# Score tiles of 32 queries and all four heads, PV packed to match, and a new hand-written order at both ends

## The chip, the cores and the metric

The kernel runs on one core of one Trainium2 chip. The metric is the time of one execution on the device in microseconds (us). Engines are named as the profile names them: PE (TensorE, matrix products), DVE (VectorE), ACT (ScalarE), POOL (GpSimd) and SP (SyncE, which here only issues transfers). The product of a 128x128 block of weights with N columns is "a matmul of N columns".

## The reference

Input `x` is (2, 512, 512): two batches, 512 tokens, 512 features. One layer follows: attention, residual and layernorm, then a feed-forward part, residual and layernorm.

```
q, k, v = x@Wq, x@Wk, x@Wv          # 32 query heads, 8 key/value heads of 128; 4 query heads share one k, v
scores  = q k^T * 128**-0.5,  causal mask,  probs = softmax(scores)
x = layernorm(x + (probs v) @ Wo)
w = sparsemax(x @ W_router^T + b_router)                       # 8 experts
x = layernorm(x + x@W_base^T + b_base + sum_e w_e (x A_e) B_e) # LoRA of rank 16 per expert
```

## The kernel before

**Precision.** Inputs and outputs are float32, and the kernel keeps nearly their precision with 16-bit products. Every operand is cut into a high part in fp16 and a low part (the rest, in fp16 too), scaled by powers of two that are found from maxima of the data. A product is then three matmuls into one PSUM tile: high x high, high x low, low x high (`mm3`, L229-232). Cutting a PSUM tile takes two instructions: ScalarE copies it to fp16 (L236), VectorE subtracts that from the original (L237).

**Groups and units.** A group is one key/value head of one batch, with its four query heads: 16 groups (g, b). A group has four units i = 0..3, one for each block of 128 queries; under the causal mask unit i needs the keys of blocks 0 to i. A unit goes through three stages:

- `unit_a` (L332): the scores, k against q. A score tile has 128 rows, which are **64 queries of two heads** (`R = P // 2`), so a unit has four tiles: heads 0 and 1 with the first 64 queries and with the last 64, then heads 2 and 3 likewise. The first sort is 128i+64 keys wide, the second 128i+128. For each tile: three matmuls into a PSUM tile of tag `S` (four buffers, so a unit fills them all); VectorE adds the mask and takes the row's extreme (L376); ScalarE takes the exponential and the row's sum (L381). After each pair of tiles `cut_p` follows: VectorE's reciprocals (L348, L350), ScalarE's high part of the normalized probabilities (L357), VectorE's low parts (L361, L363), all into the SBUF tile `phl`; then SP issues a DMA transpose of that half of `phl` to `pt` (L103). `phl` and `pt` have two buffers each, so every second unit uses the same one.
- `unit_b` (L396): PV, probabilities times v, in one PSUM tile (tag `PV`, one buffer). For the key blocks before the last, 3i matmuls of 512 columns. In the last block the first 64 queries need only 64 keys, so high and low part lie in one block of 128 rows: two matmuls of 256 columns, with copies of v packed accordingly (`vd`, `vz`); the last 64 queries take three of 256. The result is cut to `o2`.
- `unit_c` (L428): `o2` times Wo, twelve matmuls of 512 columns (`pw`), added to the accumulator `acc` by VectorE (L441).

**Between the stages.** While a group's units run, the next group's projections are computed from x: k and q of head 0 in unit 0, q1 in unit 1, v in unit 2, q2 and q3 in unit 3 (`proj`, L320). `turn_v` (L309) makes the packed copies of v on ScalarE in `v2` (4 parts of 512 columns) and transposes all 16 blocks of it in one DMA to `vt`. The cut q lies in tiles of two heads each (tag `Q`, three buffers). `factors` (L258) computes the groups' small scale factors `lm` on GpSimd.

**What sets the order.** The main loop (L899-925) calls, for unit s: `unit_a(s)`, the projections of the next group, `unit_b(s-1)`, `unit_c(s-2)`. A list `plan` (L821-851) says at which unit later weights are loaded (SP), measured (VectorE, L126, `mx`), and split (GpSimd, L120-123), and when the parts of the feed-forward block of batch 0 run (`ffn`, L643, a generator that goes on at each `step_live`). Within that, a scheduler decides each engine's order; loads on SP are held behind the third-last transpose (`hist[-3]`, L99). Each engine works through its own queue in order. Two stretches are ordered by hand instead (`tc.manual_schedule`): the **head** (L726-815), which loads x and the first weights and computes the first group's projections in float32 form before their scales are known (`park`), then their squares, maxima and scales; and the **tail** (L869), in which the last group's attention, the second batch's feed-forward block and the last block of the first batch are interleaved by the tokens of a string `TAIL` (L863). A token is a letter and a token block t: `a` scores, `p` their probabilities, `b`/`B` PV and `o`/`O` its cut, `q` a further half of the probabilities, `c`/`C` the product with Wo and `d`/`D` its sum, `n`/`N` statistics and normalizing, `x`/`X` and `l` the turn of the activations, `m` the base product (`pa`), `r` LoRA in (`pb`), `s` routing, `h` LoRA's middle (`phw`), `e` LoRA out, `f`/`F` last statistics and the store.

Of the kernel before, what the change touches and what calls it, by code (L numbers as in the profile page):

```python
# [8 lines left out]
F32 = mybir.dt.float32  # L9
F32R = mybir.dt.float32r  # L10
F16 = mybir.dt.float16
# [4 lines left out]
AX = mybir.AxisListType  # L16

P = 128
R = P // 2
NB, S, HID = 2, 512, 512  # L20
NT = S // P
KC = HID // P
NG = 8
HPG = 4
NE, NR = 8, 16
NL = NE * NR + NE
NQ = 3
SCALE = float(P) ** -0.5
NEG = -1.0e30
BIG = 3.0e38  # L30
# [11 lines left out]
def kernel(  # L42
# [33 lines left out]
    make_identity(nc, ident)  # L76
    mask = const.tile([P, S], F32, tag="mask", name="mask")
    nc.gpsimd.memset(mask, 0.0)
    for half in range(2):
        tri = mask[half * R : (half + 1) * R, S - R : S]  # L80
        nc.gpsimd.affine_select(
            out=tri, in_=tri, pattern=[[-1, R]], compare_op=ALU.is_ge, fill=NEG, base=0, channel_multiplier=1,
        )
    cmh = const.tile([P, 1], F32, tag="cmh", name="cmh")
    nc.gpsimd.memset(cmh, -0.5)
    v2 = const.tile([P, 4, S], F16, tag="v2", name="v2")
    nc.gpsimd.memset(v2[:, 3, :], 0.0)
    ones = const.tile([P, P], F32, tag="ones", name="ones")
    nc.gpsimd.memset(ones, 1.0)

# [11 lines left out]
    def sync_transpose(dst, src):  # L102
        hist.append(nc.sync.dma_start_transpose(dst, src).ins)  # L103
# [154 lines left out]
    def factors(g, b):  # L258

        lm = sb.tile([P, 8], F32, tag="lm", name=f"lm{g}_{b}", bufs=3)  # L260
        sc = SC[(g, False)]
        first = (g, b) == (0, 0)
        engine = nc.vector if first else nc.gpsimd
        engine.tensor_scalar(lm[:, 4:5], sc[:, 0, 4:5], XS[b][0], 1.0, ALU.mult, ALU.mult)  # L264

        step = 1 if first else 2
        for half in range(2):
            on = slice(half * R, (half + 1) * R)
            for p in range(0, 2, step):
                heads = slice(2 * p + half, 2 * p + half + 2 * step - 1, 2)  # L270
                engine.tensor_scalar(
                    lm[on, p : p + step], sc[on, 0, heads], lm[on, 4:5], -(2.0**-80), ALU.mult, ALU.min
                )
        LM[(g, b)] = lm

    def pj(name, tag="pj"):
# [16 lines left out]

    def end_q(g, b, h, pq):

        if h % 2 == 0:
            QT[(g, b, h // 2)] = sb.tile([P, 2, 2 * NT, 2, R], F16, tag="Q", name=f"q{g}_{b}_{h}", bufs=NQ)
        q2 = QT[(g, b, h // 2)][:, :, :, h % 2, :]
        return cut_psum(q2[:, 0], q2[:, 1], pq.rearrange("p (j q) -> p j q", q=R), cut(b, g, h))

    def mul_v(g, b, tag="pj"):
# [6 lines left out]

    def turn_v(g, b):  # L309

        first, twice = (v2[:, k : k + 2, :].rearrange("p a (t k) -> p a t k", k=P) for k in (0, 2))
        nc.scalar.copy(
            twice[:, 0].rearrange("p t (a k) -> p t a k", a=2), first[:, 0, :, :R].unsqueeze(2).broadcast_to([P, NT, 2, R])
        )
        nc.scalar.copy(twice[:, 1, :, :R], first[:, 1, :, :R])
        vt = sb.tile([P, 4 * NT, P], F16, tag="VT", name=f"vt{g}_{b}", bufs=2)
        sync_transpose(vt, v2.rearrange("p a s -> p (a s)"))
        VT[(g, b)] = vt

    def proj(g, b, j):  # L320
# [11 lines left out]
    def unit_a(g, b, i, whole=True):  # L332


        k2, lm = KT[(g, b)], LM[(g, b)]


        nb = 4 * i + 3
        phl = sb.tile([P, 2, nb * P], F16, tag="PHL", name=f"phl{g}_{b}_{i}", bufs=2)
        pt = sb.tile([P, 2, nb, P], F16, tag="PT", name=f"pt{g}_{b}_{i}", bufs=2)  # L340
        es = []
        st = sb.tile([P, 4, 4], F32, tag="ast", name=f"ast{g}_{b}_{i}", bufs=3)

        def keys(j):
            return i * P + (j + 1) * R

        def cut_p(h):
            nc.vector.reciprocal(st[:, 2, h : h + 2], st[:, 1, h : h + 2])  # L348

            nc.vector.scalar_tensor_tensor(  # L350
                st[:, 3, h : h + 2], st[:, 2, h : h + 2], 32768.0, es[h + 1][:, :2], ALU.mult, ALU.max
            )
            p = phl[:, h // 2]
            for j in range(2):
                n, src, by = keys(j), es[h + j], st[:, 3, h + j : h + j + 1]
                hi = p[:, j * (2 * i + 1) * P :][:, :n]
                nc.scalar.activation(hi, src[:, :n], AF.Copy, scale=by)  # L357
                lo = p[:, j * (2 * i + 1) * P + (i + 1) * P :][:, : i * P + j * P]
                m = lo.shape[1]
                if m:  # L360
                    nc.vector.scalar_tensor_tensor(lo, src[:, :m], by, hi[:, :m], ALU.mult, ALU.subtract)  # L361
                if m < n:
                    nc.vector.scalar_tensor_tensor(  # L363
                        p[:, n : n + R], src[:, m:n], by, hi[:, m:n], ALU.mult, ALU.subtract
                    )

            sync_transpose(pt[:, h // 2], p)

        for h in range(4):
            j = h % 2  # L370
            n, qs = keys(j), 2 * i + j
            q2 = QT[(g, b, h // 2)]
            qh, ql = (q2[:, a, qs].rearrange("p a q -> p (a q)") for a in range(2))
            sc = ps.tile([P, S], F32, tag="S", name=f"s{g}_{b}_{i}_{h}", bufs=4)
            mm3(sc[:, :n], [(qh, k2[:, 0, :n]), (qh, k2[:, 1, :n]), (ql, k2[:, 0, :n])])
            nc.vector.tensor_tensor_reduce(  # L376
                out=sc[:, :n], in0=sc[:, :n], in1=mask[:, S - n :], scale=lm[:, h // 2 : h // 2 + 1], scalar=BIG,
                op0=ALU.add, op1=ALU.min, accum_out=st[:, 0, h : h + 1],
            )

            nc.scalar.activation(  # L381
                sc[:, :n], sc[:, :n], AF.Exp, bias=st[:, 0, h : h + 1], scale=-1.0, accum_out=st[:, 1, h : h + 1]
            )
            es.append(sc)
            if whole and h % 2:
                cut_p(h - 1)
        PT[(g, b, i)] = pt
        yield
        if not whole:
            for h in (0, 2):  # L390
                cut_p(h)
                yield
# [3 lines left out]
    def unit_b(g, b, i):  # L396
        vt = VT[(g, b)]
        pt = PT.pop((g, b, i))
        pt = pt.rearrange("p e k (h q) -> p e k h q", q=R)
        pv = ps.tile([P, HPG, 2, R], F32, tag="PV", name=f"pv{g}_{b}_{i}")  # L400
        dst = pv.rearrange("p (e h) j q -> p j e h q", e=2)
        m = 2 * i + 1
        pairs = []
        for kt in range(i):
            ph, pl = (pt[:, :, k :: m][:, :, :2].rearrange("p e j h q -> p j e h q") for k in (kt, i + 1 + kt))
            vh, vl = vt[:, kt, :], vt[:, NT + kt, :]
            pairs += [(vh, ph), (vh, pl), (vl, ph)]
        if i:
            mm3(dst, pairs, last=False)

        vh, vl, vd, vz = (vt[:, k * NT + i, :] for k in range(4))
        both = pt[:, :, i]
        mm3(dst[:, 0], [(vd, both), (vz, both)], i == 0, i == 0)
        ph, pl = pt[:, :, m + i], pt[:, :, m + 2 * i + 1]
        mm3(dst[:, 1], [(vh, ph), (vh, pl), (vl, ph)], i == 0)
        yield
        o2 = sb.tile([P, 2, HPG, 2, R], F16, tag="O", name=f"o{g}_{b}_{i}", bufs=2)
        cut_psum(o2[:, 0], o2[:, 1], pv, 2.0**-15)
        OT[(g, b, i)] = o2
        yield  # L420
# [215 lines left out]
        mm3(PA[t], pairs, first=False)  # L636

    def store(t, src, st):
        y = sb.tile([P, HID], F32, tag="y", name=f"y{t}", bufs=2)
        normalize(y, src, st)  # L640
        nc.sync.dma_start(out_rows[t], y)

    def ffn(t):  # L643
# [9 lines left out]
        with behind(mybir.EngineType.PE):  # L653
            lora_in(t, False)
        route(t)
        yield
        yield
        lora_mid(t, False)
# [67 lines left out]
    with tc.manual_schedule(engines={ET.PE, ET.DVE, ET.Activation, ET.Pool, ET.SP}):  # L726
# [56 lines left out]
        end_q(0, 0, 0, PK[0])  # L783
        factors(0, 0)
        end_q(0, 0, 1, PK[1])
        for c in (2, 3):
            x_hi(1, c)
            x_lo(1, c, nc.gpsimd)
        park(2, "S")
        for c in range(KC):  # L790
            x_max(1, c)
        amax(mx[:, 7:8], mx[:, 13:17])
        end_v(0, 0, PK[5])
        park(3, "S")
        for k in range(4):
            w_squares(mx[:, 17 + k : 18 + k], wo_raw[k], "S")
        amax(sq1[:, 1:2], mx[:, 17:21])
        nc.scalar.activation(sq1[:, 0:1], mx[:, 7:8], AF.Square)
        end_q(0, 0, 2, PK[2])
        tot = total(sq1, 2, "1")  # L800
        convert = split_x(0, x0_raw)
        next(convert)
        turn_v(0, 0)
        end_q(0, 0, 3, PK[3])
        sc1 = sb.tile([P, 2, 8], F32, tag="sc1", name="sc1")
        scales(sc1, tot, 2)
        SC[(0, True)] = sc1[:, :, 1:3]
# [53 lines left out]


    TAIL = """  # L863
    n3 a7 N3 p7 B7 q7 O7 X3 l3 C6 D6 a6 r3 s3 p6 C7 q6 b7 D7 o7 h3 a5 m3 p5 q5 c7 d7 b6 n7 e3 o6
    a4 c6 N7 p4 q4 d6 X7 l7 n6 b5 m7 o5 f3 r7 c5 s7 N6 d5 h7 X6 n5 b4 e7 l6 o4 f7 F3 N5 r6 s6 F7
    c4 d4 X5 l5 n4 m6 h6 r5 m5 e6 s5 N4 f6 h5 X4 e5 l4 F6 r4 f5 s4 F5 m4 h4 e4 f4 F4
    """

    def tail():  # L869
# [112 lines left out]
```

## Time and profile before

| | |
|---|---|
| median of 3 runs | 677.68 us (677.02 to 681.1) |
| the profiled execution | 677.5 us, of which the span of its instructions is 675.4 us |
| granted TensorE clock | 0.999 of full speed |
| instructions PE / DVE / ACT / POOL | 3594 / 1698 / 1052 / 373 |
| busy DVE in 60-580 us and behind 580 us | 407.07 of 520 us, 77.68 of 96 us |
| busy PE in 60-580 us and behind 580 us | 518.36 of 520 us, 83.50 of 96 us |
| idle time of VectorE ended by a load of Wo, before a maximum (L126) | 21.6 us, 10 times |

Times are those of one execution that the hardware profiler recorded. A line that names a group of instructions gives the program's line, the engine, the operation, output <- input with shapes (partitions x elements) and the count. "Busy" of PE is not PE at its peak: the ends of matmuls are modelled and reach over the start of the next one. In lines of waits the three numbers are the idle time in all, how often, and the longest. In lines of a timeline the first two numbers are start and length in us; in square brackets stands the idle time before and what ended it.

### The profile page before, as it was taken

How to read it: one execution, taken by the hardware profiler on the slowest of the kernel's cores; microseconds unless marked ns; L12 is line 12 of the kernel's file. 1: busy time of each engine (PE TensorE's matmuls, PEld its weight loads, DVE VectorE, ACT ScalarE, POOL GpSimd, SP SyncE). 2: the span in 40 equal slices, each digit the busy share in tenths (PEclk: the TensorE clock that was granted, in tenths of full speed). 3: DMA queues.
4: the chain of work that ended last, by engine and by line, in shares of the span. 5: the costliest groups of instructions: out<-in, count | busy, mean ns of one | idle time of the engine just before them, and what ended most of it. 6: DMA issues, size and time to landing. Idle time of an engine off the chain costs nothing.

```text
span 675.4 us, 11524 instructions
## 1 busy us (share of the span) xinstructions
PE 656.8 (97%) x3594; PEld 348.6 (52%) x3594; DVE 531.6 (79%) x1698; ACT 369.5 (55%) x1052; POOL 250.3 (37%) x373
## 2 busy tenths in 40 slices
PE   8999999999999999999999999999999999999995
PEld 5755545455554545445554555555454545544452
DVE  6887788778696688678787797969777687878796
ACT  6876664746365764646464464726565465444520
POOL 4676450624117298623308067054405011100011
PEclk9999999999999999999999999999999999999999
DMA  8669393637539383635629454743726362453311
GB/s 313 203 153 164 96 192 74 147 62 131 134 68 215 92 207 59 137 70 110 156 41 207 109 104 103 151 116 73 156 44 123 40 130 47 92 117 74 71 44 47
DMA packets 205341, 78.89 MB, mean 117 GB/s; under 512 B 189920, under 2 KB 190176, under 8 KB 205280
## 3 DMA queue, kind: packets, MB, share of 16 engines
q1 hardware_dynamic: 205280, 78.17, 53.3%
q8 instruction: 28, 0.46, 0.3%
q14 instruction: 33, 0.27, 0.1%
HBM read 29.12 MB, written 2.10 MB: 46 GB/s over the span
## 4 chain that ended last, share of the span: by engine, by line
PE 74%; DVE 13%; DMA 4%; ACT 4%; issue 2%; POOL 2%; SPq 0%; POOLq 0%; ACTq 0%; DVEq 0%
PE pw L232 19%; PE pq L232 19%; PE pv L232 11%; PE s L232 11%; PE pk L232 5%; PE pvp L232 5%; PE pa L232 3%; DVE phl L361 2%; ACT s L381 2%; DVE s L376 1%; DMA raw<-in_wo_dram 1%; PE park L232 1%; DVE mx L126 1%; DVE acc L441 1%; DMA xraw<-in_xt_dram 1%
## 5 line engine op out<-in xcount | busy, mean ns | idle before, releaser
L381 ACT ACTIVATE s<-s,ast 128x192 f32<-128x192 f32 (+7 forms) x256 | 120.9, 472 | 149.8 <-DVE ast L376 143.9
L232 PE MATMUL pw<-w,o 128*128 128x512 f16 x768 | 176.9, 379 | 0.3 <-DVE o L237 0.3
L232 PEld LDWEIGHTS <-w 128*128 128x128 f16 x1008 | 98.1, 98 | 110.6
L232 PE MATMUL pq<-xT,w 128*128 128x512 f16 x672 | 152.1, 379 | 0.0
L357 ACT ACTIVATE phl<-s,ast 128x192 f16<-128x192 f32 (+7 forms) x256 | 110.7, 512 | 23.0 <-DVE ast L350 20.6
L361 DVE SCALAR_TENSOR_TENSOR phl<-s,ast,phl 128x128 f16<-128x128 f32 (+2 forms) x224 | 112.5, 515 | 8.0 <-ACT phl L357 7.4
L376 DVE CUSTOM_DVE_ANT_0 s<-s,mask,lm 128x192 f32<-128x192 f32 (+7 forms) x256 | 117.9, 519 | 0.0
L232 PEld LDWEIGHTS <-o 128*128 128x128 f16 x768 | 74.8, 98 | 77.2 <-DVE o L237 1.0
L232 PE MATMUL s<-k,q 128*128 128x320 f16 (+7 forms) x768 | 106.6, 286 | 3.3 <-DVE phl L363 1.9
L232 PE MATMUL pv<-pt,vt 128*128 128x256 f16 (+1 forms) x608 | 107.7, 323 | 1.5 <-DMA pt<-phl 1.0
L232 PEld LDWEIGHTS <-q 128*128 128x128 f16 x768 | 64.2, 98 | 45.1 <-DVE phl L363 3.3
L264 POOL TENSOR_SCALAR lm<-sc,xs 128x1 f32<-128x1 f32 x15 | 4.0, 267 | 220.6 <-DVE sc L140 111.5
L232 PEld LDWEIGHTS <-vt 128*128 128x128 f16 x608 | 59.2, 99 | 50.4 <-issue 2.0
L123 POOL TENSOR_TENSOR w<-raw,w 128x512 f16<-128x512 f32 x70 | 79.6, 1157 | 0.3
L441 DVE SCALAR_TENSOR_TENSOR acc<-pw,lm,acc 128x512 f32<-128x512 f32 x64 | 47.7, 745 | 22.8 <-PE pw L232 22.5
L120 POOL TENSOR_SCALAR raw<-raw,sc 128x512 f32<-128x512 f32 x70 | 47.9, 694 | 47.0 <-issue 36.2
L237 DVE SCALAR_TENSOR_TENSOR o<-pv,o 128x512 f16<-128x512 f32 x64 | 43.8, 684 | 24.8 <-ACT o L236 24.8
L126 DVE TENSOR_REDUCE mx<-raw 128x1 f32<-128x512 f32 x68 | 44.4, 677 | 21.6 <-DMA raw<-in_wo_dram 21.6
L236 ACT ACTIVATE o<-pv 128x512 f16<-128x512 f32 x64 | 39.5, 617 | 37.3 <-PE pv L232 37.1
L381 ACT ACTIVATION_READ_ACCUMULATOR s<-s,ast 128x1 f32 x256 | 51.3, 200 | 0.0
L237 DVE SCALAR_TENSOR_TENSOR q<-pq,q 128x512 f16<-128x512 f32 x56 | 37.9, 683 | 10.7 <-ACT q L236 10.4
L236 ACT ACTIVATE q<-pq 128x512 f16<-128x512 f32 x56 | 34.1, 614 | 21.2 <-PE pq L232 21.1
(170 smaller groups left out, 652.5 us busy)
## 6 DMA issues: line engine op xcount, KB each, us to landing
raw<-in_wo_dram SPq DMA_DIRECT2D x32, 256.0 KB, 3.9
raw<-in_wq_dram SPq DMA_DIRECT2D x29, 256.0 KB, 4.2
xraw<-in_xt_dram SPq DMA_DIRECT2D x8, 256.0 KB, 5.2
raw<-in_wk_dram SPq DMA_DIRECT2D x8, 256.0 KB, 3.5
raw_x<-in_xt_dram SPq DMA_DIRECT2D x8, 256.0 KB, 4.9
acc<-in_x_dram SPq DMA_DIRECT2D x8, 256.0 KB, 5.1
pt<-phl SPq DMA_TRANSPOSE x128, 3.6
out_dram<-y SPq DMA_DIRECT2D x8, 256.0 KB, 2.0
```

What stands on the lines that cost most here:

```text
L120: nc.gpsimd.tensor_scalar(view, view, by, 1.0, ALU.mult, ALU.mult)
L123: return first.ins, nc.gpsimd.tensor_tensor(lo, view, hi, ALU.subtract).ins
L126: nc.vector.tensor_reduce(dst, view, AX.X, ALU.max, apply_absolute_value=True)
L232: nc.tensor.matmul(dst, a, b, start=first and j == 0, stop=last and j == n - 1)
L236: nc.scalar.activation(hi, psrc, AF.Copy, scale=by)
L237: return nc.vector.scalar_tensor_tensor(lo, psrc, by, hi, ALU.mult, ALU.subtract).ins
L264: engine.tensor_scalar(lm[:, 4:5], sc[:, 0, 4:5], XS[b][0], 1.0, ALU.mult, ALU.mult)
L357: nc.scalar.activation(hi, src[:, :n], AF.Copy, scale=by)
L361: nc.vector.scalar_tensor_tensor(lo, src[:, :m], by, hi[:, :m], ALU.mult, ALU.subtract)
L376: nc.vector.tensor_tensor_reduce(out=sc[:, :n], in0=sc[:, :n], in1=mask[:, S - n :], scale=lm[:, h // 2 : h // 2 + 1], scalar=BIG, op0=ALU ...
L381: nc.scalar.activation(sc[:, :n], sc[:, :n], AF.Exp, bias=st[:, 0, h : h + 1], scale=-1.0, accum_out=st[:, 1, h : h + 1])
L441: nc.vector.scalar_tensor_tensor(a, pw, LM[(g, b)][:, 7:8], a, ALU.mult, ALU.add)
```

## The change

**Score tiles.** `R` is now 32. A score tile has the **32 queries of all four heads** in its 128 rows, and the four tiles of a unit are four successive blocks of 32 queries, 128i+32, +64, +96 and +128 keys wide. All heads' q go into one tile (tag `Q`, two buffers), and the four scale factors, which were two columns for two pairs of heads, are one column written in four quarters of the partitions: two operations more on GpSimd.

**Probabilities.** `phl` and `pt` become one tile each of 4m+2 blocks of 128 columns, with m = 2i+1. The first two tiles of a unit share the last key block: tile 0 has 32 keys there, written three times by ScalarE beside one low part; tile 1 has 64 keys high and 64 low. Tiles 2 and 3 have a whole block for high and for low each; the 32 columns that tile 2 does not fill in these two are zeroed by a ScalarE copy at the start of `unit_a`. A unit still has two transposes, of 2m and of 2m+2 blocks (before: 2m+1 each).

**V and PV.** `v2` has a fifth part, with v's first 32 keys of a block for the fourfold packing, and two more ScalarE copies fill it; its transpose has 20 blocks instead of 16. PV takes 3i matmuls of 256 columns for tiles 0 and 1, one of 128 columns for tile 0's last keys, two of 128 for tile 1's, and 3(i+1) of 256 for tiles 2 and 3.

**Orders.** In the head, `park(2)` and `park(3)` and the cuts of q2 and q3 stand elsewhere, and the squares of Wo are taken in two pairs. In the first group of each batch V's transpose is held behind the last transpose issued. `ffn` has one `yield` more before LoRA's middle. The stored result takes buffers of tag `rawo`. `TAIL` has a new order.

```diff
-R = P // 2
+R = P // 4
-    v2 = const.tile([P, 4, S], F16, tag="v2", name="v2")
+    v2 = const.tile([P, 5, S], F16, tag="v2", name="v2")
...
+        for h in range(HPG):
+            on = slice(h * R, (h + 1) * R)
+            engine.tensor_scalar(lm[on, 0:1], sc[on, 0, h : h + 1], lm[on, 4:5], -(2.0**-80), ALU.mult, ALU.min)
...
-        if h % 2 == 0:
-            QT[(g, b, h // 2)] = sb.tile([P, 2, 2 * NT, 2, R], F16, tag="Q", name=f"q{g}_{b}_{h}", bufs=NQ)
-        q2 = QT[(g, b, h // 2)][:, :, :, h % 2, :]
+        if h == 0:
+            QT[(g, b)] = sb.tile([P, 2, HPG * NT, HPG, R], F16, tag="Q", name=f"q{g}_{b}", bufs=2)
+        q2 = QT[(g, b)][:, :, :, h, :]
...
     def turn_v(g, b):
+        nc.scalar.copy(twice.rearrange("p t (a k) -> p t a k", a=2), double(2, r))
+        nc.scalar.copy(once[:, :, :r], low[:, :, :r])
+        nc.scalar.copy(four.rearrange("p t (a k) -> p t a k", a=4)[:, :, ::3], double(2, R))
+        nc.scalar.copy(four[:, :, R:r], low[:, :, :R])
+        vt = sb.tile([P, 5 * NT, P], F16, tag="VT", name=f"vt{g}_{b}", bufs=2)
+        with tc.issue_after(hist[-1]) if g == 0 and hist else nullcontext():
+            sync_transpose(vt, v2.rearrange("p a s -> p (a s)"))
...
     def unit_a(g, b, i, whole=True):
+        m = 2 * i + 1
+        nb = 4 * m + 2
+        phl = sb.tile([P, nb * P], F16, tag="PHL", name=f"phl{g}_{b}_{i}", bufs=2)
+        nc.scalar.copy(
+            phl.rearrange("p (k a) -> p k a", a=P)[:, 2 * m + i : 2 * m + m + 1 : i + 1, 3 * R :],
+            mask[:, : 2 * R].rearrange("p (k a) -> p k a", k=2),
+        )
...
+                if j > 1:
+                    high(p[:, :n], src[:, :n])
+                    low(lows[:, :n], 0, n)
+                    continue
+                if j:
+                    high(p[:, :n], src[:, :n])
+                else:
+                    if i:
+                        high(p[:, :full], src[:, :full])
+                    high(
+                        p[:, full : full + 3 * R].rearrange("p (a k) -> p a k", a=3),
+                        src[:, full:n].unsqueeze(1).broadcast_to([P, 3, R]),
+                    )
+                if i:
+                    low(lows[:, :full], 0, full)
+                low(p[:, full + (3 - j) * R : full + P][:, : n - full], full, n - full)
+            on = slice(0, 2 * m) if h == 0 else slice(2 * m, nb)
+            sync_transpose(pt[:, on], phl[:, on.start * P : on.stop * P])
...
+        for j in range(4):
+            n = full + (j + 1) * R
+            qh, ql = (q2[:, a, HPG * i + j].rearrange("p h q -> p (h q)") for a in range(2))
...
     def unit_b(g, b, i):
+        for kt in range(i):
+            pairs += three(kt, 0, m)
         if i:
-            mm3(dst, pairs, last=False)
+            mm3(dst[:, :2], pairs, last=False)
+        mm3(dst[:, 0], [(four, p0)], i == 0, i == 0)
+        mm3(dst[:, 1], [(twice, p1), (once, p1)], i == 0)
+        pairs = []
+        for kt in range(i + 1):
+            pairs += three(kt, 2 * m, m + 1)
+        mm3(dst[:, 2:], pairs)
...
-        y = sb.tile([P, HID], F32, tag="y", name=f"y{t}", bufs=2)
+        y = sb.tile([P, HID], F32, tag="rawo", name=f"y{t}", bufs=4)
...
         route(t)
         yield
         yield
+        yield
         lora_mid(t, False)
...
         end_q(0, 0, 1, PK[1])
+        park(2, "S")
         for c in (2, 3):
             x_hi(1, c)
             x_lo(1, c, nc.gpsimd)
-        park(2, "S")
+        park(3, "S")
+        for k in range(2):
+            w_squares(mx[:, 17 + k : 18 + k], wo_raw[k], "S")
         for c in range(KC):
             x_max(1, c)
         amax(mx[:, 7:8], mx[:, 13:17])
+        end_q(0, 0, 2, PK[2])
         end_v(0, 0, PK[5])
-        park(3, "S")
-        for k in range(4):
+        for k in (2, 3):
             w_squares(mx[:, 17 + k : 18 + k], wo_raw[k], "S")
         amax(sq1[:, 1:2], mx[:, 17:21])
         nc.scalar.activation(sq1[:, 0:1], mx[:, 7:8], AF.Square)
-        end_q(0, 0, 2, PK[2])
         tot = total(sq1, 2, "1")
+        end_q(0, 0, 3, PK[3])
...
-        end_q(0, 0, 3, PK[3])
...
     TAIL = """
-    n3 a7 N3 p7 B7 q7 O7 X3 l3 C6 D6 a6 r3 s3 p6 C7 q6 b7 D7 o7 h3 a5 m3 p5 q5 c7 d7 b6 n7 e3 o6
-    a4 c6 N7 p4 q4 d6 X7 l7 n6 b5 m7 o5 f3 r7 c5 s7 N6 d5 h7 X6 n5 b4 e7 l6 o4 f7 F3 N5 r6 s6 F7
-    c4 d4 X5 l5 n4 m6 h6 r5 m5 e6 s5 N4 f6 h5 X4 e5 l4 F6 r4 f5 s4 F5 m4 h4 e4 f4 F4
+    n3 a7 C6 N3 B7 p7 q7 O7 X3 l3 D6 a6 r3 C7 s3 b7 p6 q6 D7 h3 o7 m3 a5 p5 c7 b6 q5 e3 d7 o6 n7
+    a4 c6 N7 p4 q4 b5 f3 X7 l7 m7 o5 r7 d6 n6 s7 c5 N6 d5 h7 X6 n5 l6 b4 e7 o4 f7 r6 c4 N5 F7 s6
+    F3 X5 l5 d4 n4 m6 h6 r5 m5 s5 N4 e6 f6 h5 X4 l4 F6 e5 r4 s4 f5 m4 h4 F5 e4 f4 F4
     """
```

## The prediction

> **What bounds the kernel.** I read the page's first part, then the chain that ended last, then TensorE's instructions in order of time over one steady group, then what TensorE waited for.
>
> ```profile
> PE 656.8 (97%) x3594; PEld 348.6 (52%) x3594; DVE 531.6 (79%) x1698; ACT 369.5 (55%) x1052; POOL 250.3 (37%) x373
> PE 74%; DVE 13%; DMA 4%; ACT 4%; issue 2%; POOL 2%; SPq 0%; POOLq 0%; ACTq 0%; DVEq 0%
> ```
>
> TensorE is busy for 97% of the span and carries 74% of the chain; VectorE (79%) is next. The clock is granted in full. The group from 200.21 us, in order of time (start, length, engine, line, matmul, count):
>
> ```profile
> 200.21 2.59 PE L232 MATMUL s<-k,q 128*128 128x448 f16 x12
> 202.64 5.34 PE L232 MATMUL pq<-xT,w 128*128 128x512 f16 x24
> 207.82 2.00 PE L232 MATMUL pv<-pt,vt 128*128 128x512 f16 x11
> 209.66 2.75 PE L232 MATMUL pw<-w,o 128*128 128x512 f16 x12
> 212.25 0.67 PE L232 MATMUL s<-k,q 128*128 128x64 f16 x12
> 212.76 2.75 PE L232 MATMUL pk<-xT,w 128*128 128x512 f16 x12
> ...
> 217.94 2.65 PE L232 MATMUL pv<-pt,vt 128*128 128x512 f16 x14
> 220.43 2.75 PE L232 MATMUL pw<-w,o 128*128 128x512 f16 x12
> ...
> 226.76 0.71 PE L232 MATMUL pv<-pt,vt 128*128 128x256 f16 x5
> 227.31 2.75 PE L232 MATMUL pw<-w,o 128*128 128x512 f16 x12
> ```
>
> Lengths hold the pipeline's end, so I go from start to start: the scores of unit 3 (5,760 columns) take 202.64 - 200.21 = 2.43 us, those of unit 0 (1,152 columns) 0.51 us. That is 1.92 us for 4,608 columns, **0.417 ns a column**, and (510 - 480) / 12 = **2.5 ns a matmul**. Nothing else: no row waits for its weights. A 512-column matmul is then 216 ns, and twelve are the 2.59 us of pw. So in the middle of the run the time is a sum of columns. The waits that TensorE does have:
>
> ```profile
> PE s L232 <- DVE phl L363: 1.9, 4, 1.1
> PE phw L628 <- DVE hw L619: 1.6, 2, 1.4
> PE px L567 <- DVE phl L363: 1.3, 1, 1.3
> ...
> PE tot L131 <- ACT q L236: 1.1, 1, 1.1
> PE s L232 <- DVE q L237: 1.0, 1, 1.0
> PE pv L232 <- DMA pt<-phl: 1.0, 1, 1.0
> ```
>
> Nearly all lie in the first 60 us and behind 580 us; between, some 2 us, most at 289 us.
>
> **Scores.** Unit i had tiles of 128i+64 and 128i+128 columns, each twice, three matmuls to a tile: 13,824 columns in a group of four units. Now it has 128i+32, +64, +96, +128: 13,056. The count stays at 48. -768 x 0.417 = -0.32 us a group. The 32-column matmul has no row before: between 16 ns (by the two rates) and 29 ns (the 64-column one, 64 x 0.417 + 2.5). [...] **-0.29 us a group.**
>
> **PV.** Before, 3i matmuls of 512 and five of 256: 14,336 columns, 38 matmuls in a group. Now 3i of 256, one and two of 128 for the packed last keys, 3(i+1) of 256: 13,824 columns, 60 matmuls. -512 x 0.417 + 22 x 2.5 ns = -0.21 + 0.06 = **-0.16 us a group.** Sum -0.45, times 16 groups: **-7.2 us**, and the path runs through it.
>
> [...]
>
> **Other engines, steady part.** VectorE: mask and low parts lose 64 columns each a unit, about 0.13 us by its rows (619 to 754 ns for 384 to 512 columns, 1.05 ns a column): -0.5 us a group, same count. ScalarE gains a high part in three of four units (the 96-column copy, near the 371 ns row of 128 columns, about 0.27 us of its own time), a 128x64 copy of zeros in each unit (nearest row 317 ns at 64 columns) and two copies a group for V (409 and about 330 ns): 3 x 0.3 + 4 x 0.27 + 0.7 = 2.7 us, less 0.5 for narrower tiles. 55% becomes about 61%: costs nothing by itself. GpSimd gets two more small operations a group (295 ns), hidden at 37%.
>
> **New order of waits.** (a) Each score tile now needs all four heads, so the first needs what the third needed: 0.26 us earlier. The cover is PV and pw, 4.4 us; in most groups the last q is done 2.9 us ahead, but not in groups that prepare weights:
>
> ```profile
> 201.22 2.72 SPq L103 DMA_TRANSPOSE vt<-v  x1
> 207.08 0.69 DVE L126 TENSOR_REDUCE mx<-raw 128x1 f32<-128x512 f32 x1 [3.09 <-DMA raw<-in_wo_dram]
> 211.75 0.68 DVE L237 SCALAR_TENSOR_TENSOR q<-pq,q 128x512 f16<-128x512 f32 x1
> ```
>
> A maximum waits on VectorE for Wo's load, which stands on SP's queue behind V's transpose; the last q follows at 212.43, scores start at 212.25. V's transpose grows from 16 to 20 blocks: 2.72 / 4 = +0.7 us on SP, for the loads and the unit's own transposes behind it. Against it, in the built order of the changed program one of the two maxima between the low parts has gone behind the last q (0.6 us), and the low parts are 0.1 shorter. Net 0, and the 0.26 remains in six or so groups, 1.6 us, of which VectorE's lighter load of 0.5 us a group should take the larger part: between -1.5 (the stall at 289 goes) and +4, I take **+0.5 us**.
>
> (b) ScalarE's copy of zeros waits for the transposes of two units earlier, and stands ahead of exponentials. For unit 0 the exponentials began at 215.70 and the transpose in question landed at 217.26; over the groups that is 0 to 4.4 us, about 1.9. Behind it on ScalarE stand that unit's exponentials, high parts, k and q; for them wait VectorE's cuts, then the next unit's scores for PSUM. Those begin at 223.02, the cuts ended at 220.0: 3.0 us of cover here (3.3 to 5.8 elsewhere). I take 0; if cover were gone it is the first rival.
>
> **Beginning.** In the first group the scores also wait for head 3, whose cut now follows the second sum's squares; the sum's matmul waits about 1.2 us longer (VectorE finishes the maxima and two cuts first), and VectorE's v and q cuts stand ahead of it. Against that, all four tiles are ready together, the cut of the second half no longer waits behind a maximum for w1 (0.97 us), and the 1.0 us that PV waited for its transpose is mostly covered, since pvp is whole and one score ahead of it. **-0.5 us** (-1.5 to +1.5).
>
> **End.** By the new order the nine pvp matmuls (1.9 us) come ahead of phw (wait 1.4), PV ahead of pa (0.4), pw ahead of px (1.25; pw is 2.6), thirteen pa ahead of the scores that waited 1.1, and the last routing ahead of statistics (0.2). That is 4.4 us of TensorE waits. But from 603 us VectorE carries the chain, and pa moved behind seven PV matmuls is 1.0 us later in its line while VectorE waits 2.89 us for it at 605.94. So I count 1.4 + 0.4 - 1.0 = 0.8 for the first two, nothing for the next two, 0.5 for VectorE's smaller tiles in six units, and 0.2 for the routing: 0.8 + 0.5 + 0.2 = **-1.5 us** (0 to -4.4). The store's buffer change costs nothing: those raw buffers are long read.
>
> **Sum.** The profiled execution took 677.5 us, 675.4 of span and 2.1 around it; the median of the runs is 677.68, the same. 677.5 - 7.2 + 0.5 - 0.5 - 1.5 = **668.8 us**.
>
> **Rivals.**
> *Slower: ScalarE's queue becomes the bound.* The zeros' copy holds exponentials until a transpose lands that is itself 0.7 us later, on an engine with 2.2 us more work a group. It decides from where the delay, 1.9 us on average, passes the 3 us cover at unit 1's scores. In its favour: one group has 4.4 us. Against it: the groups with long delays have 5.8 us of cover. If 15 groups lost 1.2 us each, 668.8 + 18 = 686.8 us. It is slower as soon as the loss passes 0.6 us a group. 8%.
> [...] 6%.
> *The orders bring nothing* and (a) costs its upper end: 677.5 - 7.2 + 2 = 672.3 us, between 670.5 and 674. 23%.
> *The end gains all it can*, and the 289 us stall goes: 677.5 - 7.2 - 1 - 1 - 4 = 664.3 us. 15%.
> *The change doesn't do what it says*: the order shows the new widths and counts, so hardly.
>
> **Chances.** The forecast (666 to 670.5) has 48%. About 1% of the time is what a measurement can tell: below 670.9 is faster. 48 + 15 + 10 of the third rival's 23 give 0.73 faster, 13 + 6 give 0.19 within, 0.08 slower. The range that leaves out a fifth: 663.5 to 674.5.
>
> **What would show it.** A group's period falls from 38.0 to about 37.5 us. Start to start, scores take about 0.46 / 1.07 / 1.71 / 2.35 us by unit and PV 0.50 / 1.15 / 1.80 / 2.46. [...] If TensorE's waits name VectorE's low parts or q at each group's start, and ScalarE shows idle time ahead of the copy of zeros ended by a transpose, the first rival holds. TensorE's waits behind 580 us fall by 2 to 4 us if the new end works. I am wrong if some engine writes the 32-element runs of q, or TensorE PSUM's 32-column runs, slower than the 64-element ones of before; nothing in the trace speaks of it.

## The result and the profile after

The changed kernel is **slower**: 708.94 us (median of 6, 704.85 to 709.86) against 677.56 us before (6 runs), ratio 1.0444, 95% interval 1.0409 to 1.0478. The forecast was 668.8 us. The sign is that of the first rival (ScalarE's queue), which had been given 8% and 686.8 us.

The profiled execution took 709.86 us, 707.7 of span. Of its page, the busy times and the chain that ended last:

```profile
PE 664.8 (94%) x3946; PEld 376.0 (53%) x3946; DVE 521.2 (74%) x1698; ACT 386.9 (55%) x1196; POOL 258.5 (37%) x405
PE 16%; DVE 12%; ACT 7%; DMA 6%; issue 2%; POOL 1%; POOLq 0%; ACTq 0%; DVEq 0%; SPq 0%
```

TensorE's share falls from 97% to 94%. The chain, which could be followed over less than half of the span here, no longer runs along TensorE alone: DMA has 6%, and its costliest step is `pt<-phl`, the transpose of the probabilities. What TensorE waited for (idle time in us, times, longest):

```profile
PE s L231 <- DVE q L236: 12.9, 8, 2.6
PE s L231 <- ACT q L235: 5.2, 6, 1.9
PE s L231 <- DVE phl L368: 4.7, 11, 0.9
PE pq L231 <- DVE q L236: 2.9, 1, 2.9
```

Before, these sums were 1.0 us for q and 1.9 for phl. The scores wait for q, the projections too, since q's PSUM is not read in time. And what ScalarE waited for, the two longest entries:

```profile
ACT phl L347 <- DMA pt<-phl: 164.0, 52, 8.1
...
ACT s L400 <- DVE ast L395: 70.3, 36, 7.2
```

L347 is the new copy of zeros. Before, no transpose stood in the list, and its first entry was the exponentials' ordinary wait for VectorE:

```profile
ACT s L381 <- DVE ast L376: 143.9, 60, 4.7
```

Here is the group that the prediction showed, ScalarE in order of time (start, length, and in brackets the idle time before and what ended it):

```profile
205.88 0.24 ACT L347 CAST phl<-mask 128x64 f16<-128x64 f32 x1 [1.89 <-DMA pt<-phl]
206.03 0.47 ACT L400 ACTIVATE s<-s,ast 128x288 f32<-128x288 f32 x1
...
209.99 0.65 ACT L235 ACTIVATE v<-pvp 128x512 f16<-128x512 f32 x1
...
213.68 0.58 ACT L400 ACTIVATE s<-s,ast 128x416 f32<-128x416 f32 x1 [1.24 <-DVE ast L395]
...
215.69 0.24 ACT L347 CAST phl<-mask 128x64 f16<-128x64 f32 x1 [1.31 <-DMA pt<-phl]
215.84 0.60 ACT L400 ACTIVATE s<-s,ast 128x448 f32<-128x448 f32 x1
...
217.76 2.47 ACT L365 ACTIVATE phl<-s,ast 128x384 f16<-128x384 f32 x5
220.07 1.13 ACT L235 ACTIVATE q<-pq 128x512 f16<-128x512 f32 x2
```

The copy stands ahead of unit 2's exponentials (206.03) and again between the first two of unit 3 (215.84), each time ended by the landing of the transposes that read the same phl buffer. Both traces have a landmark in this group, the small `tot` sum on TensorE. Here it and the first exponential of unit 2, from the trace before, and the landmark in the changed kernel:

```profile
194.03 0.50 ACT L381 ACTIVATE s<-s,ast 128x320 f32<-128x320 f32 x1 [1.63 <-DVE ast L376]
196.29 0.28 PE L131 MATMUL tot<-sq,ones 128*128 128x6 f32 x2
```

```profile
205.22 0.28 PE L130 MATMUL tot<-sq,ones 128*128 128x6 f32 x2
```

Counted from the landmark, unit 2's exponentials start 3.1 us later than before (0.81 us behind it, where they were 2.26 us ahead), and everything behind them on ScalarE follows: v, its copies, V's transpose, q2 and q3. On TensorE:

```profile
218.96 2.75 PE L231 MATMUL pw<-w,o 128*128 128x512 f16 x12
221.55 0.20 PE L231 MATMUL s<-k,q 128*128 128x32 f16 x2
224.36 0.87 PE L231 MATMUL s<-k,q 128*128 128x32 f16 x10 [2.61 <-DVE q L236]
225.02 4.18 PE L231 MATMUL pk<-xT,w 128*128 128x512 f16 x12
229.04 2.75 PE L231 MATMUL pq<-xT,w 128*128 128x512 f16 x12
```

Two things are to be seen. The scores wait 2.61 us for q. And the twelve matmuls of pk that follow take 4.02 us from start to start where twelve are worth 2.59 us. The same stretches with the granted clock (third figure from the end; window, its length, then busy time of each engine):

```profile
221.50:224.40 2.90, 0.29 (x5) 0.14 (x4) 2.90 (x7) 0.19 (x1) 2.90 (x5) 1.00 0.47 91
225.00:229.10 4.10, 4.10 (x16) 1.63 (x14) 3.28 (x13) 0.24 (x1) 1.21 (x2) 0.65 1.00 204
```

**The sum.** Priced from start to start (2.4 ns and 0.417 ns a column, the float32 forms by their own rows), all matmuls of before are worth 649.2 us and those of after 641.5. From the first matmul's start to the last one's end, TensorE took 668.4 us and 700.6. So the change took away 7.7 us of work, as the prediction said, and put 40.0 us of lost time in (19.0 before, 59.0 after, the last matmul left out): about 29 us in single waits above 0.25 us and about 8 us in matmuls behind such waits, where the granted clock is 0.50. These sums price a 32-column matmul at 16 ns, by the two rates; in the changed kernel's trace it takes 25 ns. With that, the work taken away is 7.3 us and the lost time after is 0.4 us smaller.

### The profile page after: what moved, and what is told of

It is laid out like the page before. It is cut to its first block, busy times and chain, and to the rows that moved or that the text cites. A ratio compares the mean times of both kernels' runs of the same rounds, so it can differ in the third digit from the quotient of the medians.

```text
span 707.7 us, 12374 instructions
## 1 busy us (share of the span) xinstructions
PE 664.8 (94%) x3946; PEld 376.0 (53%) x3946; DVE 521.2 (74%) x1698; ACT 386.9 (55%) x1196; POOL 258.5 (37%) x405
## 5 line engine op out<-in xcount | busy, mean ns | idle before, releaser
L231 PEld LDWEIGHTS <-w 128*128 128x128 f16 x1008 | 99.9, 100 | 118.9 <-issue 11.6
L400 ACT ACTIVATE s<-s,ast 128x320 f32<-128x320 f32 (+15 forms) x256 | 117.1, 457 | 73.3 <-DVE ast L395 70.3
L368 DVE SCALAR_TENSOR_TENSOR phl<-s,ast,phl 128x128 f16<-128x128 f32 (+7 forms) x352 | 124.9, 417 | 17.5 <-ACT phl L365 15.0
L231 PE MATMUL s<-k,q 128*128 128x480 f16 (+15 forms) x768 | 105.8, 282 | 23.7 <-DVE q L236 12.9
L365 ACT ACTIVATE phl<-s,ast 128x96 f16<-128x96 f32 (+11 forms) x304 | 117.2, 480 | 7.5 <-DVE ast L355 6.7
L395 DVE CUSTOM_DVE_ANT_0 s<-s,mask,lm 128x320 f32<-128x320 f32 (+15 forms) x256 | 113.4, 503 | 2.7 <-PE s L231 2.7
L347 ACT CAST phl<-mask 128x64 f16<-128x64 f32 x64 | 15.7, 247 | 176.6 <-DMA pt<-phl 164.0
L231 PEld LDWEIGHTS <-q 128*128 128x128 f16 x768 | 62.2, 99 | 68.7 <-DVE q L236 14.1
L231 PEld LDWEIGHTS <-vt 128*128 128x128 f16 x960 | 86.2, 99 | 22.9 <-issue 4.5
L353 DVE RECIPROCAL ast<-ast 128x2 f32<-128x2 f32 x128 | 21.0, 164 | 93.6 <-ACT s L400 93.1
L125 DVE TENSOR_REDUCE mx<-raw 128x1 f32<-128x512 f32 x68 | 44.0, 677 | 11.7 <-DMA raw<-in_wo_dram 11.6
L231 PE MATMUL pk<-xT,w 128*128 128x512 f16 x168 | 44.1, 417 | 0.0
```

The costliest lines, as they stand in the source:

```text
L125: nc.vector.tensor_reduce(dst, view, AX.X, ALU.max, apply_absolute_value=True)
L231: nc.tensor.matmul(dst, a, b, start=first and j == 0, stop=last and j == n - 1)
L347: nc.scalar.copy(phl.rearrange("p (k a) -> p k a", a=P)[:, 2 * m + i : 2 * m + m + 1 : i + 1, 3 * R :], mask[:, : 2 * R].rearrange("p (k a ...
L365: nc.scalar.activation(dst, src, AF.Copy, scale=by)
L368: nc.vector.scalar_tensor_tensor(dst, src[:, at : at + k], by, p[:, at : at + k], ALU.mult, ALU.subtract)
L395: nc.vector.tensor_tensor_reduce(out=sc[:, :n], in0=sc[:, :n], in1=mask[:, S - n :], scale=lm[:, 0:1], scalar=BIG, op0=ALU.add, op1=ALU.mi ...
```

## The experiments

"W" in the expectations is the theory that the copy's wait ahead of the exponentials makes the loss. Each result stands beside the kernel before in runs of the same series (676.7 to 677.3 us); bracketed pairs are intervals of the ratio to it.

### Is it the copy's wait?

**The copy moved.** In `unit_a`, its emission goes from the start into `cut_p`:

```diff
-        nc.scalar.copy(phl..., mask...)            # at the start of unit_a
+            if h == 2:                              # in cut_p
+                with tc.issue_after(last[0]) if whole else nullcontext():
+                    zeros()                         # last[0]: the unit's last exponential
```

> The changed kernel, with ScalarE's copy of zeros into phl moved behind the unit's own four exponentials (just ahead of the high parts, which wait for the same buffer anyway); the order of all other work stays as in the changed kernel but for a handful of neighbours. Theory W (the copy's wait for a transpose, standing ahead of the next unit's exponentials, holds back exponentials, V's transpose, Wo's loads, maxima, q and so the scores): the idle time of ScalarE ended by a pt transpose ahead of the copy falls from 164 us to under 30 us, TensorE's waits for q from 18 us to under 4 us, and the time is 667 to 673 us. Rival V (V's transpose of 20 blocks and the two further V copies do it): 700 us or more. Rival M (the small matmuls cost more than their columns): 700 us or more, with the waits gone all the same.

Measured 674.32 us, 0.9961 (0.9949 to 0.9973): 34.6 us back with one instruction moved, and no transpose among ScalarE's waits for the copy. TensorE's waits:

```profile
PE s L231 <- DVE q L236: 3.0, 4, 1.3
PE pv L231 <- DMA pt<-phl: 1.6, 3, 0.9
PE s L231 <- ACT q L235: 1.6, 1, 1.6
```

Those for q came to 4.8 us with the smaller rows, 0.8 more than expected, and the time is 1.3 us above the expected range: something is left, and a later section takes it up.

**The copy alone, in the kernel before:**

```diff
+        nc.scalar.copy(phl[:, :, :32], mask[:, :64].rearrange("p (k a) -> p k a", k=2))
```

> The kernel before, with one added ScalarE copy of 2x32 zeros a unit into the first columns of both halves of phl, at the start of unit_a (the high parts overwrite it later, so the result is unchanged); it comes to stand ahead of the next unit's exponentials just as in the changed kernel. Own time 64 x 0.25 = 16 us of ScalarE. Theory W: the whole loss appears without any of the change, 677.5 + 25 to 38 = 702 to 715 us. Rivals V and M, or the orders: 677 to 681 us.

Measured 700.38 us, 1.0353 (1.0328 to 1.0377). It writes nothing that lasts, and it costs 23.6 us, a little under the expected range. ScalarE's first waits of this kernel:

```profile
ACT phl L343 <- DMA pt<-phl: 128.0, 48, 6.2
ACT s L382 <- DVE ast L377: 75.7, 38, 4.4
```

So a loss of two thirds of this size (23.6 of 34.6 us) needs neither small matmuls nor the larger V.

**Form and orders apart.** The changed kernel with the old head, tail, yields and hold:

> The changed kernel with the old orders: head, tail, routing's yields and the hold on V's transpose as before the change (the result's buffers stay). Theory W: still slow, 704 to 713 us, as the copy stands where it stood. Rival O (the new orders do the harm): 669 to 680 us.

711.92 us (1.049 to 1.054). The new orders alone on the old form:

> The kernel before with the new orders alone (head, tail, one more yield, hold on V's transpose, result's buffers). Theory W: within 3 us of before, 674.5 to 679 us; by the prediction's two terms 677.5 - 0.5 - 0.7 = 676.3 us. Rival O: 690 us or more.

673.73 us, 0.9962 (0.995 to 0.9973), a little under the expected range: the orders gain 3.1 us. And the new form without the copy's wait, under the old orders:

> The changed kernel with the copy of zeros behind the exponentials, and with the old orders of head and tail, the old yields, and no hold on V's transpose: the new form alone, without the copy's wait. If the orders are worth what they were worth on the kernel before (677.6 to 673.7, about 3 us): 674.3 + 3 = 677 us (675.5 to 679), so the form by itself would be worth nothing although TensorE's sum of columns is 7.7 us smaller, and the waits for q at the groups' starts must make up for it. If the orders gain nothing in the new form: 674 us.

678.68 us, 1.0038 (1.0024 to 1.0051). On the new form the orders are thus worth 4.4 us (678.7 - 674.3). The form alone costs 2 us even without the wait, although its matmuls are worth 7.7 us less.

**Another engine for the zeros:** `nc.gpsimd.memset` in place of the copy.

> The changed kernel with the zeros written by GpSimd (a memset of the same 2x32 columns) instead of ScalarE; nothing else is edited. The wait for the transposes then stands on GpSimd's queue, among the splits of the weights. Theory W: ScalarE's exponentials no longer wait for a transpose, TensorE's waits fall as with the late copy, 671 to 678 us. If the loss hung on ScalarE's added work rather than on its wait, the gain over the late copy (16 us less of ScalarE) shows as 671 us or less; if GpSimd's own queue becomes the holder, 680 us or more.

675.96 us (0.9971 to 0.9994). The wait is still there, on a queue where it holds up little that TensorE needs:

```profile
POOL phl L347 <- DMA pt<-phl: 145.8, 29, 13.7
```

This frees ScalarE of 16 us of work beside the late copy and gains nothing: its work was not the matter, its order was.

### By which way does it reach TensorE?

In the group shown, a maximum waits for Wo's load behind V's transpose (1.48 us, up to 219.74 us), and q, cut from 223.02 us on, waits behind that maximum. Two runs loosened that link with the copy left early. First the maxima, held behind earlier VectorE work (`behind(DVE)` for Wo's rows too):

> The changed kernel as it is, with the copy of zeros ahead of the exponentials, but Wo's maxima held behind the earlier VectorE work. Theory W1 (the delay reaches TensorE by way of V's transpose, Wo's loads, a maximum and q): most of the loss goes, 676 to 690 us. Theory W2 (it reaches TensorE by the exponentials themselves: late high and low parts, late PSUM and late q on ScalarE): 695 us or more.

705.8 us. It is no clean cut, since a new wait came: the sum over the late maxima now held TensorE itself.

```profile
PE tot L130 <- ACT sq L188: 10.3, 5, 2.9
PE s L231 <- DVE phl L368: 5.7, 7, 3.1
PE s L231 <- DVE q L236: 4.8, 5, 1.2
```

The cleaner one, Wo's loads one unit earlier (`u - 2` for `u - 1` in `plan`):

> The changed kernel, copy of zeros ahead of the exponentials as it is, with Wo's loads planned one unit earlier. Theory W1 (the delay reaches TensorE through V's transpose, Wo's loads, a maximum and q): 680 to 695 us. Theory W2 (late exponentials delay high parts, low parts and q directly): 700 us or more.

706.93 us. By the medians that is 2 us, which the intervals (1.0404 to 1.0463, against 1.0409 to 1.0478 of the changed kernel) do not tell from nothing. The link is not gone everywhere: VectorE's idle time ended by Wo's loads, ahead of a maximum, fell from 11.6 us to 6.6. But in the group shown no load stands before q any more, and TensorE still waits 1.16 us for it (2.61 with the link). So in that group the link made a part of the wait; that the exponentials' own followers (high parts, low parts, q and v) carry most of the loss is argued from this, not tried by itself.

### At which of its places?

The scheduler had put each unit's copy one unit ahead. From the trace of the changed kernel, ScalarE's idle time ahead of the copies: before unit 0's exponentials 62 us, before unit 1's 35, before unit 2's 41, before or inside unit 3's 21, behind 580 us 18. Not all of that is loss, as the exponentials might not have been ready. The mean time from the start of a unit's first mask to the start of its first exponential, over the thirteen groups of the main loop behind the first, tells more: before 0.47, 0.51, 0.70 and 0.77 us for units 0 to 3, after 2.48, 0.49, 1.82 and 1.09. So the copy before unit 1 held nothing up; those before 0 and 2 did, and in unit 3 the last exponential ends 8.4 us after the first score (4.9 before).

Putting copies back one place at a time went only partly as planned, since the scheduler and the two buffers moved with them. Three runs can be read. In the first, unit 3's copy landed in a harmless place (ahead of unit 3's exponentials), so of the main loop it tests the place inside unit 3 only (in the tail, copies of units 0 and 3 were early too, and TensorE's lost time there was as with late ones, 7.0 us against 6.9):

> The late copy of zeros, but the copies of unit 3 (ahead of unit 2's exponentials, behind unit 1's transposes) and of the next unit 0 (between the first two exponentials of unit 3, behind unit 2's transposes) put back: the two places that the prediction did not price. If these carry the loss, since unit 3's exponentials end 3.5 us later and q2 and q3 are cut behind them: 690 to 705 us. If unit 0's place carries it: 674 to 679 us. If each costs on its own and they add up, this one and the run with unit 0's place together lose 35 us.

679.32 us, +5.0 over the late copy. And all places of the main loop, the tail's copies late:

> The changed kernel as it is in its main loop, all copies at the places they have there, and only the hand-ordered tail with the copies behind the exponentials. Behind 580 us the changed kernel's TensorE idles 12.0 us, with late copies 7.0 us. If the tail carries that difference: 709 - 5 = 704 us (702 to 706). If it is the main loop's doing: 708 to 710 us.

705.97 us: by the medians the tail is worth 3.0 us, which the intervals (1.039 to 1.0487, against 1.0409 to 1.0478) do not tell from nothing. In between stands the run with the places ahead of unit 0 and inside unit 3, in which unit 3's copy was again not ahead of unit 2:

> The late copy of zeros, but with the copies of units 0, 1 and 3 back where the changed kernel has them, all three places at once (the earlier two runs put back one and two of them and lost 4.7 and 5.0 us); unit 2's copy, ahead of unit 1's exponentials, and those of the hand-ordered tail stay late. If the delays add up one by one: 674.3 + 9.7 = 684 us (681 to 687). If they compound, because exponentials, transposes and the next exponentials then stand in one row through three units and the sum passes the cover that each alone stays under: 695 us or more, with 25 us or more of TensorE waits between 60 and 580 us.

686.86 us. ScalarE's waits for the transposes, from the runs with one, two and all places, in a fence each:

```profile
ACT phl L348 <- DMA pt<-phl: 26.5, 13, 3.6
```

```profile
ACT phl L351 <- DMA pt<-phl: 94.9, 26, 8.2
```

```profile
ACT phl L348 <- DMA pt<-phl: 157.9, 49, 7.8
```

Added in this order, the place inside unit 3 costs 5.0 us, the one ahead of unit 0 7.5 (686.86 - 679.32), those ahead of units 1 and 2 together 19.1 (705.97 - 686.86), the tail 3.0. In the run with two places the mean from mask to exponential was 0.53 us for unit 1 and 0.69 for unit 2, as before the change; with all of them it is 0.49 and 1.82. So by these means the 19.1 us fall to the place ahead of unit 2, where v, its copies and V's transpose stand behind the exponentials; no run put the two places apart. These are prices in company, from medians of four runs that lie up to 6.6 us apart; another order of adding could share them out otherwise.

Three more runs were meant for single places and do not test them:

> The late copy of zeros, but unit 1's copy put back ahead of unit 0's exponentials, where it waits for unit 3's last transpose: the one place that the prediction priced (at 0, with 3 us of cover). If that place carries the loss: 690 to 705 us. If the prediction was right on this place and the loss sits at the others: 674 to 679 us.

> The late copy of zeros, but unit 3's copy put back ahead of unit 2's exponentials, where it waits for unit 1's transposes. The two earlier runs that were to have it there had it ahead of unit 3's exponentials instead, where its wait is long over, so that this place has not been tried. If it carries what is missing (709 us with all copies early, 687 us with those ahead of units 0 and 3): 690 to 697 us. If the places compound, it costs no more than the others by itself: 676 to 682 us.

> The late copy of zeros, but unit 2's copy put back ahead of unit 1's exponentials, behind unit 0's transposes, which land 3.7 us before those exponentials begin: the last of the four places by itself. If each place has a price of its own, this one must carry what is missing: 706 (all four) - 687 (two of them) - 0 (ahead of unit 2) = 19 us, so 690 us or more. If the places compound: 673 to 676 us.

Measured 679.04, 673.67 and 677.34 us. To get the copy ahead, phl was allocated a unit early, and by where the waits went this swapped its two buffers: idle time ahead of the copies was 2.6, 0.0 and 5.6 us in all. In the first, unit 0's high parts waited for the transposes instead (18.1 us), behind the exponentials. My reading of the second as a place without a price, on which the last expectation was built, falls with that. A place by itself was not tried for units 0, 1 and 2.

### What is left with the late copy

With the late copy TensorE loses 9.1 us between 60 and 580 us, against 3.5 before. VectorE at one group's start in that run:

```profile
287.91 0.69 DVE L125 TENSOR_REDUCE mx<-raw 128x1 f32<-128x512 f32 x1 [3.96 <-DMA raw<-in_wo_dram]
288.51 2.77 DVE L374 SCALAR_TENSOR_TENSOR phl<-s,ast,phl 128x384 f16<-128x384 f32 x6
291.20 1.28 DVE L236 SCALAR_TENSOR_TENSOR q<-pq,q 128x512 f16<-128x512 f32 x2
```

All six low parts and both q now stand behind one maximum that waits for a load. Three ways to take that away, on top of the late copy. A transpose of 16 blocks:

> The late copy of zeros, and V's transpose back at 16 blocks: the fourfold part of v is still written but not transposed, and PV reads the twofold part in its place (the first 32 queries of every block of 128 then get a wrong weight of their last keys). Theory V2 (the larger transpose delays Wo's loads on SP, those delay a maximum on VectorE, and that delays q): TensorE's waits for q (4.8 us with the late copy alone) fall under 2 us, the time to 670 to 672 us. Rival Q (the scores wait because a tile now needs all four heads, whatever the load does): waits above 3.5 us, 673 to 675 us.

675.58 us. The waits for q fell to 3.3 us, others (phl 3.0, o 2.4) came. Later maxima:

> The late copy of zeros, and Wo's maxima on VectorE held behind the VectorE work that was emitted before them, so that they no longer stand ahead of the last low parts and q. If the waits for q that are left (4.8 us) come from a maximum waiting for Wo's load: they vanish, 668 to 671 us, below both kernels. If they come from elsewhere: 673 to 676 us.

676.19 us; waits of the sum over the maxima came instead (`PE tot <- ACT sq`, 2.9 us in 5). Wo's loads a unit earlier:

> The late copy of zeros, and Wo's loads planned one unit earlier, so that the first of the four stands ahead of V's transpose on SP instead of behind it. With the late copy alone TensorE idles 9.1 us between 60 and 580 us (3.5 before the change). If the q at the groups' starts is late because the maximum ahead of it waits for that load (3.0 to 4.0 us each time): that sum falls to about 5 us and the time to 669 to 672 us. If, as with the smaller transpose and the later maxima, another wait takes its place: 673 to 676 us.

674.47 us: the four waits for q near 137, 213, 291 and 368 us had gone, and new ones had come near 402 and 482 us, in the groups that prepare weights 6 and 7, whose places in `plan` differ. So the last run moved the loads for the others only:

```diff
-            at(prepare(g, ROWS), u - 1, u, u + 1, ...)
+            at(prepare(g, ROWS), u - (2 if g < NG - 2 else 1), u, u + 1, ...)
```

> The late copy of zeros, and Wo's loads planned one unit earlier for weights 2 to 5 only. In the run that did it for all, the four waits for q near 137, 213, 291 and 368 us (3.6 us in all) had gone, and new ones had come near 402 and 482 us (4 us), in the two groups of weights 6 and 7. If the waits are separate: 674.3 - 3.6 = 670.7 us (669.5 to 672), below both kernels. If others take their place: 673 to 675 us.

**670.59 us** (670.26 to 671.35), 0.9906 (0.9887 to 0.9925): faster than both kernels, than the one before by 1%. TensorE loses 4.7 us between 60 and 580 us, and VectorE's q no longer appears among its first waits:

```profile
PE s L231 <- ACT q L235: 1.4, 1, 1.4
PE pv L231 <- DMA pt<-phl: 1.2, 2, 0.9
```

With the copy and these loads moved, the form and the orders come within 1.8 us of the forecast. What the earlier loads alone would give the kernel before, whose maxima also wait for them, was not run; so the whole 6.2 us against it cannot be put down to the form and the orders.

## The prediction, step by step

**Columns (-7.2): right.** The sum of all matmuls fell by 7.7 us by the two rates, by 7.3 with the 32-column one at its 25 ns; the quiet groups went from 38.0 to 37.5 us. Start to start, the 32-column matmul takes 25 ns in the changed kernel's trace where nothing holds it, the one of 64 columns 28, of 96 columns 42, of 128 columns 56, in scores and in PV. The scores' -0.29 us a group, where the columns alone give -0.32, and the 0.46 us of unit 0 rest on a price of about 25 ns for the 32-column matmul that the trace before does not show, since it has none; the changed kernel's showed 25 ns. The other small ones are within 1 ns of the two rates.

**(b), the copy of zeros (0): the step that failed**, by 34.6 us. It had the wait and its first-order size: at unit 0 the exponentials were to be held 1.9 us, and they were, from 0.47 to 2.48 us behind the mask. Two things were wrong. The first is the path from there to TensorE. The prediction followed the delay to unit 1's scores, with 3.0 us of cover, and there the cover held: no score of unit 1 waits in the changed kernel's trace. But q2 and q3 are cut behind unit 3's exponentials on the same queue, and all 14 waits of scores for q, 18.1 us, stand at the scores of unit 0, at a group's start. The second is that it looked at one place of four; the copies ahead of unit 2 and inside unit 3 stand on the same ScalarE queue, and these and the tail make 27 of the 34.6 us by the order of adding above. The transposes of units 1 and 2 land in before's trace only 0.3 us after the next unit's first exponential and 1.4 after unit 3's second, so from means they look cheap; but a held exponential makes the next transposes late, and those hold the next exponentials. (That they add up along this ring is argued; no run had the place ahead of unit 2 by itself.) And the mean delay of 1.9 us hid the long ones: unit 0's first exponential came up to 5.1 us behind its mask, and unit 0's place makes 7.5 of the 34.6 us by the same order of adding.

**(a), all four heads for the first score (+0.5): mis-sized.** With the late copy, 60 to 580 us lost 5.6 us more than before (9.1 - 3.5), above the bound of 4. With Wo's loads moved it is 1.2 (4.7 - 3.5). The term was the maximum ahead of all low parts and q: the prediction let one maximum's move behind q and VectorE's lighter load cancel it, but the maximum that waits for the load stayed in front.

**Beginning (-0.5) and end (-1.5).** With the late copy TensorE lost 8.2 us in the first 60 us (6.8 before) and 7.0 behind 580 us (8.8 before): +1.5 and -1.8. The end is right; in the head, on the upper bound, part of the loss is half-speed matmuls behind waits of 1.56 and 0.91 us that ended at 25.60 and 26.76 us (in the changed kernel's trace the same two waits are 1.51 and 0.91 us, and the granted clock is 0.50 from 26.52 to 29.93 us).

With these terms, 677.5 - 7.7 + 5.6 + 1.5 - 1.8 = 675.1 us for the late copy, whose profiled execution took 675.24. The first rival named the cause, and its signs are what the trace shows: waits for q at the groups' starts, and ScalarE idle ahead of the copy until a transpose lands. But its way to TensorE was unit 1's scores too, and its 1.2 us a group was a guess below the 31.7 us that the main loop's copies cost (705.97 - 674.32), 2 us a group.

## What to carry to other kernels

The copy of zeros, which overwrites phl, waited 52 times and 164.0 us in all for the transposes that read the same buffer. Place an instruction that overwrites a buffer where its engine would wait for that buffer's last reader anyway, and not ahead of work that is ready. In a built order, look at every place where a new wait stands, follow the delay to everything behind it on that engine's queue, add the delays along the ring that they form, and compare the longest of them, not the mean, with the cover. When a wait is removed, ask what is late next: of the four runs that took the maximum's wait away on top of the late copy, three brought others of nearly the same size.

## What the runs showed of the hardware

A wait of TensorE could cost more than its own length here, since the granted clock was lower behind some of them. In the changed kernel's trace the clock is 1.00 or 0.50 from 6.04 us on, and all moments at which it changes lie whole multiples of 3.413 us apart (between 60 and 580 us it falls at 101.61, 224.49, 309.82 and 466.83 us, which are 36, 25 and 46 such stretches, called windows here). Two pairs of windows from that trace (TensorE's busy time is the first figure behind the length, the clock the third from the end):

```profile
221.08:224.49 3.41, 0.80 (x10) 0.43 (x9) 3.41 (x8) 0.61 (x2) 3.41 (x6) 1.00 0.51 111
224.49:227.90 3.41, 3.41 (x17) 1.59 (x16) 3.41 (x12) 0.00 (x0) 1.72 (x2) 0.50 1.13 212
384.91:388.32 3.41, 2.14 (x12) 0.98 (x10) 3.32 (x8) 2.04 (x5) 3.41 (x5) 1.00 0.59 203
388.32:391.74 3.42, 2.12 (x18) 1.21 (x19) 3.42 (x7) 0.00 (x0) 3.21 (x4) 1.00 1.08 201
```

The first window holds the wait of 2.61 us, and the next one is granted 0.50. TensorE is busy in all of its 3.41 us, so that half of its length, 1.7 us, is lost. Another wait, of 2.57 us, ended at 389.62 us; a window's end cuts it in two, into 1.27 us (3.41 - 2.14) and 1.30 us (3.42 - 2.12), and the clock stays at 1.00. In the new orders on the old form, two waits of 0.88 and 1.04 us fell into one window, and the next was granted 0.50.

```profile
288.43:291.84 3.41, 1.49 (x15) 0.84 (x12) 3.41 (x7) 1.42 (x3) 2.84 (x4) 1.00 0.91 172
291.84:295.25 3.41, 3.41 (x9) 1.21 (x8) 2.92 (x15) 1.73 (x11) 0.00 (x0) 0.50 0.62 117
```

In the changed kernel's trace, up to the last matmul, the windows at 1.00 in which TensorE was idle for 1.96, 2.12, 2.37, 2.61 and 3.03 us were each followed by one at 0.50. The others had at most 1.55 us, and none of them was. In the trace before no window had more than 1.38 us up to the last matmul, and the clock stayed at 1.00 from 4.55 us to 673.56.
